# Layer 0's first sample in its own PSUM banks and TensorE's order as written: convolution attention, gated scan attention and expert layer on one core

## The chip, the cores and the metric

One core of a Trainium2 chip runs the whole kernel. The metric is device time in microseconds (us) of that core, lower is better. The median of three runs stands for a kernel; a profiled execution is one further run with the hardware profiler on, and has a time of its own.

## The reference, cut to what matters

The input is `x` of shape (4, 128, 64, 64): four samples, 128 channels, 4096 positions. Layer 0 is an attention over positions whose queries, keys and values come from 1x1 convolutions of the group-normed input:

```python
v = group_norm(x)                                  # 32 groups, over the whole sample
e1 = prelu(w1 @ v + b1)      # (4, 64, 4096)
e2 = prelu(w2 @ v + b2)      # (4, 64, 4096)
asm = prelu(wa @ v + ba)     # (4, 128, 4096)
score = softmax(einsum('nci,ncj->nij', e1, e2), axis=2)
x = x + einsum('nij,ncj->nci', score, asm)
```

Layer 1 takes the positions as tokens `t`: `t = t + attn(norm(t))`, where attn is a running softmax over time with 8 heads (keys and values are `silu` of projections, scores are key times a fixed query per head, outputs are cumulative sums divided by cumulative weights, averaged over heads); then `t = t + ffn(norm(t))`, where 64 experts each pick their 8 best tokens per sample, pool them, and run a two-layer network whose result is added back to the picked tokens. All is in float32.

## The kernel before

**Layer 0.** A sample is cut into 8 query blocks of 512 positions (`BLK`). For each block `qb` there are 16 steps `p`; a step handles 256 key positions as two halves of 128. Three functions make a step: `probs` multiplies keys by queries into a PSUM tile `sc` (two banks), ScalarE exponentiates it to `pr` and VectorE adds `pr` to the running sums `acc`; `weigh` multiplies the values `am` by `pr` into two accumulators `av`. Scores contract over 64 rows, and `weigh` splits its 128 rows in two halves, so both use half of the PE array each and run two at a time. The loop over `steps` issues `probs` of the next step ahead of `weigh` of the present one. After 16 steps `collect` copies `av` out (L604 on ScalarE, L605 on VectorE), and the next block's step 9 calls `finish`.

**Preparation of a sample.** `preparation(b)` returns work for one sample: `stat` (statistics of 512 columns, L442), `chain0` to `chain2` (group means and roots, by two tiny matmuls with `gavg`), and for each block k of 512 columns `normal` (xn, L470), `project` and `value`. `project(k)` multiplies the normed block by both small weights (L495), then biases it on ScalarE (L501, y), takes the PReLU in parts (L478 or L482, L483, L484) to `ee`, and sends it by four copies (L513, L514) to the tiles `e1` (queries of block k) and `e2` (keys of blocks' steps 2k and 2k+1). `value(k)` does eight matmuls of 128 columns (L525), adds the bias on VectorE (L537, ya), and takes the PReLU to `am` (L482 and L483 on ScalarE, L484 on VectorE). The three later samples are prepared inside the loop, one piece at steps 2, 6 and 10 of a query block, from half-array matmuls. The first sample is prepared in the open: the input comes in four transfers of 512 KB (L391) on the queues of SP and ScalarE in turn, two blocks are prepared before the first step, and blocks 2 to 7 inside the first query block, block p/2 + 2 at each even step p, ahead of the step's `weigh`. For this sample `project` and `value` share one PSUM tile `whole` of two banks, out of the pool `ps_x`:

```python
if not whole:
    whole.append(ps_x.tile([P, 2, BLK], F32, tag="x", name=f"whole_{b}"))
pe = whole[0]
nc.tensor.matmul(pe[:, 0, :], w12, xn, start=True, stop=True)
```

`value` takes `whole[0][:, 1:]`. [...]

**What sets the order.** Every engine runs its instructions in a fixed order. A planner chooses that order when the program is built: among instructions whose inputs it takes to be ready, it goes by the order of the source, so work that is ready early moves ahead. `tc.issue_after(i)` puts what it encloses behind instruction i on i's engine. `tc.manual_schedule(engines={PE})` gives TensorE the source's order for what it encloses; before, that held for the last step of layer 0 and for layer 1, and all the rest of layer 0 was left to the planner. Waits for data and for buffers are added by the framework: a tile is handed on when all that reads it has finished.

**Layer 1.** A loop over 32 blocks of 512 tokens, in TensorE's written order. `keys` makes one 128x512 projection per head (L361) into a PSUM tile of the pool `ps_kv`, which has three banks, and ScalarE applies Silu (L362); `scan` takes the running maximum, an Exp on ScalarE (L839), the running sum and a reciprocal; `weights` transposes the scan's result (L880); `values` makes the value projections through the same three banks (L916, L920); `totals` and `outputs` write to the pools `ps_t` and `ps_o`, two banks each. In block 0 the second half of the keys of block 1 (heads 4 to 7) is computed after `scan(0)` has begun and before `weights(0)`. The expert layer comes last.

Of the kernel before, what the change touches and what calls it, by code (L numbers as in the profile page):

```python
# [8 lines left out]
F32 = mybir.dt.float32  # L9
AF = mybir.ActivationFunctionType  # L10
ALU = mybir.AluOpType
AX = mybir.AxisListType
PSUM = bass.MemoryType.PSUM
P = 128
# [4 lines left out]
def conv_attn_hybrid_kernel(  # L19
# [23 lines left out]
    nc = tc.nc  # L43
    B, C, N = x.shape
    R = w1t.shape[1]
    NH = qt.shape[1]
# [4 lines left out]
    BLK = 512  # L51
# [10 lines left out]
    def opener(stack, pre=""):  # L62
        def open_pool(name, bufs=1, **kw):
            return stack.enter_context(
                tc.tile_pool(name=pre + name, bufs=bufs, reuse_waits="tile", **kw)
            )
        return open_pool
# [286 lines left out]
            nc.tensor.transpose(ptr[:, c // 2, :, c % 2, :], xl, ident)  # L354
        return nc.scalar.copy(xt, ptr.rearrange("p q s u j -> p (q s u j)")).ins

    def keys(n, xt, heads, kss, ps, pre=""):

        for h in heads:
            pk = ps.tile([P, BLK], F32, tag="kv", name=f"{pre}pk_{n}_{h}")  # L360
            nc.tensor.matmul(pk, wks[:, h, :], xt, start=True, stop=True)  # L361
            nc.scalar.activation(kss[h], pk, AF.Silu)  # L362
        return [kss[h] for h in heads]
# [8 lines left out]
    with ExitStack() as l0:  # L372
# [7 lines left out]
        wp = pool("l0w")  # L380
        tmp = pool("l0tmp", 2)
        small = pool("l0small", 2)
        ps_x = pool("l0x", space=PSUM)
        ps_av = pool("l0av", space=PSUM)
        qs_p = pool("l0q", NBLK + 1)

        def load_x(b, queues):
            xs = one.tile([P, N], F32, tag="x", name=f"x_{b}")
            for q in range(4):
                cols = bass.ts(q, N // 4)  # L390
                queues[q % len(queues)].dma_start(out=xs[:, cols], in_=x[b, :, cols])  # L391
            return xs

# [28 lines left out]

        gavg = wp.tile([P, P], F32, tag="gavg", name="gavg")
        make_block_diagonal(nc, gavg, C // 32)
        nc.vector.tensor_scalar_mul(gavg, gavg, 32.0 / C)

        queries, keys_of, values_of, sent = {}, {}, {}, []

        def preparation(b):
# [11 lines left out]
            def stat(k):  # L441
                nc.vector.bn_stats(stats[:, k, :], xs[:, bass.ts(k, BLK)])  # L442

            def chain0():
                nc.vector.bn_aggr(mv, stats)

            def chain1():
                pg = ps_x.tile([P, 2, BLK], F32, tag="x", name=f"pg_{b}")
                nc.tensor.matmul(pg[:, 0, 0:1], gavg, mv[:, 0:1], start=True, stop=True)
                nc.vector.tensor_copy(gst[:, 0:1], pg[:, 0, 0:1])  # L450
                nc.vector.tensor_sub(gst[:, 1:2], mv[:, 0:1], gst[:, 0:1])
                nc.vector.scalar_tensor_tensor(
                    out=gst[:, 2:3], in0=gst[:, 1:2], scalar=gst[:, 1:2], in1=mv[:, 1:2],
                    op0=ALU.mult, op1=ALU.add,
                )

            def chain2():
                pg = ps_x.tile([P, 2, BLK], F32, tag="x", name=f"pg2_{b}")
                nc.tensor.matmul(pg[:, 0, 0:1], gavg, gst[:, 2:3], start=True, stop=True)
                i = nc.scalar.activation(std[:, 0:1], pg[:, 0, 0:1], AF.Sqrt, bias=eps5)  # L460
                nc.vector.reciprocal(std[:, 1:2], std[:, 0:1])
                return i.ins

            xn_of = {}

            whole = []

            def normal(k):
                xn = prep.tile([P, BLK], F32, tag="xn", name=f"xn_{b}_{k}")
                nc.vector.tensor_scalar(  # L470
                    out=xn, in0=xs[:, bass.ts(k, BLK)], scalar1=gst[:, 0:1],
                    scalar2=std[:, 1:2], op0=ALU.subtract, op1=ALU.mult,
                )
                xn_of[k] = xn

            def prelu(dst, y, z, minus_a, negative):
                if negative is nc.vector:
                    nc.vector.tensor_scalar(  # L478
                        out=z, in0=y, scalar1=-1.0, scalar2=0.0, op0=ALU.mult, op1=ALU.max
                    )  # L480
                else:
                    nc.scalar.activation(z, y, AF.Relu, scale=-1.0)  # L482
                nc.scalar.activation(y, y, AF.Relu)  # L483
                nc.vector.scalar_tensor_tensor(  # L484
                    out=dst, in0=z, scalar=minus_a, in1=y, op0=ALU.mult, op1=ALU.add
                )

            def project(k):

                xn = xn_of[k]  # L490
                if b == 0:
                    if not whole:
                        whole.append(ps_x.tile([P, 2, BLK], F32, tag="x", name=f"whole_{b}"))
                    pe = whole[0]
                    nc.tensor.matmul(pe[:, 0, :], w12, xn, start=True, stop=True)  # L495
                else:
                    pe = ps_x.tile([P, 2, BLK], F32, tag="x", name=f"pe_{b}_{k}")
                    for u, h in enumerate(halves):
                        nc.tensor.matmul(pe[:, u, :], w12[h, :], xn[h, :], start=True, stop=True)
                y = prep.tile([P, BLK], F32, tag="y", name=f"y_{b}_{k}")  # L500
                nc.scalar.activation(y, pe[:, 0, :], AF.Identity, bias=b12)  # L501
                if b > 0:
                    nc.vector.tensor_add(y, y, pe[:, 1, :])
                z = prep.tile([P, BLK], F32, tag="z", name=f"z_{b}_{k}")
                ee = prep.tile([P, BLK], F32, tag="ee", name=f"ee_{b}_{k}")
                prelu(ee, y, z, neg[:, 0:1], nc.vector if (b, k) == (0, 0) else nc.scalar)
                e1 = qs_p.tile([P, BLK], F32, tag="e1", name=f"e1_{b}_{k}")
                queries[b, k] = e1

                queues = (nc.sync, nc.scalar) if (b, k) == (0, 0) else (nc.sync, nc.sync)  # L510
                by = ee.rearrange("r (j u p) -> r j u p", u=2, p=P)
                for u, (h, queue) in enumerate(zip(halves, queues)):
                    queue.dma_start(out=e1[h, :], in_=ee[halves[0], :])  # L513
                    moved = queue.dma_start(  # L514
                        out=e2[h, bass.ts(k, CPB // 2), :], in_=by[halves[1], :, u, :]
                    )
                if (b, k) != (0, 0):
                    sent.append(moved.ins)

            def value(k):  # L520
                xn = xn_of[k]
                if b == 0:
                    pa = whole[0].rearrange("p u (c d) -> p u c d", c=CPB)[:, 1:]
                    for c in range(CPB):
                        nc.tensor.matmul(  # L525
                            pa[:, 0, c, :], xn[:, bass.ts(c, P)], was, start=True, stop=True
                        )
                else:
                    pa = ps_x.tile([P, 2, CPB, C], F32, tag="x", name=f"pa_{b}_{k}")
                    for c in range(CPB):  # L530
                        for u, h in enumerate(halves):
                            nc.tensor.matmul(
                                pa[:, u, c, :], xn[h, bass.ts(c, P)], was[h, :],
                                start=True, stop=True,
                            )
                y = prep.tile([P, CPB, C], F32, tag="y", name=f"ya_{b}_{k}")
                nc.vector.tensor_tensor(  # L537
                    y, pa[:, 0], bas.unsqueeze(1).to_broadcast([P, CPB, C]), ALU.add
                )
                if b > 0:  # L540
                    nc.vector.tensor_add(y, y, pa[:, 1])
                z = prep.tile([P, CPB, C], F32, tag="z", name=f"za_{b}_{k}")
                prelu(am[:, bass.ts(k, CPB), :], y, z, neg[:, 1:2], nc.scalar)

            first = [lambda k=k: stat(k) for k in range(NBLK)] + [chain0]
            chain = [chain1, chain2]
# [6 lines left out]
        def work_off(blocks, n):  # L553
            for pre, f in blocks[:n]:
                pre()
                f()
            del blocks[:n]
# [100 lines left out]
        with tc.issue_after(root):  # L658
            nc.scalar.activation(seed[:, 1:2], eps5, AF.Exp)
        own = blocks  # L660
        work_off(own, 4)
        nxt = probs(*steps[0])
        first_sums(0, 0, nxt)
# [2 lines left out]
        end = l0.enter_context(ExitStack())  # L666
        for n, (b, qb, p) in enumerate(steps):
            pr = nxt
            if own and p % 2 == 0:
                work_off(own, 2)  # L670
                if not own:
                    with tc.issue_after(sent[-1]):
                        xs_of[1] = load_x(1, (nc.sync,))
            if n + 1 < len(steps):
                nxt = probs(*steps[n + 1])
            if n + 2 == len(steps):
# [3 lines left out]
                for i in range(2):  # L680
                    last_turned = turned(i, xls[i], xts[i], early_room[1])
            weigh(b, qb, p, pr)

            q0 = 1 if b == 0 else 0
            if (qb, p) == (q0, 0) and b + 1 < B:
# [80 lines left out]
    def layer1(pre, ready):  # L766
# [6 lines left out]
        with ExitStack() as kept, ExitStack() as l1:  # L773
# [337 lines left out]
            def loop():  # L1111
# [8 lines left out]
                for n in range(NB):  # L1120
# [7 lines left out]
                    if n + 2 < NB:  # L1128
                        xls = tokens(n + 2, xl_place)
                    if n == 0:  # L1130
                        ks += keys(n + 1, xt_of[n + 1], range(NH // 2, NH), kss, ps_kv, pre)
                    es, rr, _ = made
                    ems = weights(n, es)
                    if n >= 2:
# [391 lines left out]
```

## Time and profile before

| what | us |
|---|---|
| median of three runs (2395.74 to 2397.02) | 2396.14 |
| the profiled execution's own time | 2395.19 |
| its span, first to last instruction | 2393.5 |
| first score matmul (L567) starts | 24.96 |
| copy of the first query block's result (L604) starts | 87.37 |
| end of a query block without preparation to the next one's | 42.53 |
| TensorE idle before the key of head 5 of block 1 (L361) | 2.02 |

The profile's rows give a start and a duration in us, the engine, the source line, what is written from what, and in brackets how long the engine had been idle and what ended that. "PE" rows are matmuls, "PEld" rows are weight loads; every float32 matmul of the source shows as two instructions (x2). SPq and ACTq are the issues of DMAs on those queues. In tables of windows the columns are: window, its length, busy time of PE, PEld, DVE, ACT and POOL with instruction counts, the granted TensorE clock, the DMA share and GB/s.

### The profile page before, as it was taken

The numbers are of one execution on the slowest core, as the hardware profiler recorded it, in microseconds if no ns is written. First come the engines' busy times: TensorE is split into PE (matmuls) and PEld (weight loads), VectorE is DVE, ScalarE is ACT, GpSimd is POOL, SyncE is SP. The second block draws the span as 40 slices with busy tenths as digits, with TensorE's granted clock in tenths as the row PEclk, the third lists the DMA queues.
The fourth block names the chain that finished last, engine by engine and source line by source line (L and its number), as shares of the span: only waits on it lengthen the run. The fifth ranks groups of instructions, "written<-read, shape, count | busy, mean of one in ns | idle before, by whom it ended". The sixth has DMA issues, their size and how long they took to land.

```text
span 2393.5 us, 45621 instructions
## 1 busy us (share of the span) xinstructions
PE 2347.4 (98%) x19416; PEld 1556.4 (65%) x19416; DVE 1493.6 (62%) x2594; ACT 1208.1 (50%) x1639; POOL 301.4 (13%) x337
## 2 busy tenths in 40 slices
PE   7999999999999999999999999999999999999887
PEld 3467767677778677778777775555555555655553
DVE  5666666666655666655555556666666677776655
ACT  5454444444443444444443435666666666666541
POOL 0000000000000000000000001343343433333300
PEclk9999999999999999999999999999999999999999
DMA  3200020001110000020000000212112121112388
GB/s 81 75 23 14 23 62 1 12 18 23 49 25 1 12 18 23 14 56 1 1 1 1 1 1 19 55 38 52 41 38 55 38 51 42 38 38 55 118 309 318
DMA packets 61189, 109.93 MB, mean 46 GB/s; under 512 B 10032, under 2 KB 35120, under 8 KB 60976
## 3 DMA queue, kind: packets, MB, share of 16 engines
q1 hardware_dynamic: 57536, 101.22, 14.7%
q10 hardware_dynamic: 3440, 5.70, 0.7%
q8 instruction: 154, 2.52, 0.4%
q14 instruction: 59, 0.48, 0.1%
HBM read 85.40 MB, written 8.91 MB: 39 GB/s over the span
## 4 chain that ended last, share of the span: by engine, by line


## 5 line engine op out<-in xcount | busy, mean ns | idle before, releaser
L592 PE MATMUL av<-pr,am 64*128 64x512 f32 x4096 | 1066.2, 591 | 0.0
L571 ACT ACTIVATE pr<-sc 128x1024 f32<-128x1024 f32 x512 | 523.2, 1022 | 676.5 <-PE sc L567 607.7
L574 DVE TENSOR_TENSOR acc<-acc,pr 128x1024 f32<-128x1024 f32 x480 | 586.7, 1222 | 440.4 <-ACT pr L571 440.3
L592 PEld LDWEIGHTS av<-pr,am 64*128 64x128 f32 x4096 | 637.8, 187 | 260.3 <-issue 46.8
L567 PE MATMUL sc<-e,e 64*128 64x512 f32 x2048 | 629.3, 593 | 0.0
L567 PEld LDWEIGHTS sc<-e,e 64*128 64x128 f32 x2048 | 320.2, 187 | 107.6 <-issue 24.5
L361 PE MATMUL pk<-room,wks 128*128 128x512 f32 x512 | 241.1, 610 | 2.6 <-ACT room L362 2.4
L916 PE MATMUL pv<-wvs,room 128*128 128x512 f32 x512 | 226.4, 595 | 2.3 <-ACT v L920 2.3
L920 ACT ACTIVATE v<-pv 128x512 f32<-128x512 f32 x256 | 152.5, 597 | 69.9 <-PE pv L916 69.9
L362 ACT ACTIVATE room<-pk 128x512 f32<-128x512 f32 x256 | 148.0, 597 | 56.7 <-PE pk L361 56.4
L916 PEld LDWEIGHTS pv<-wvs,room 128*128 128x128 f32 x512 | 97.0, 191 | 121.0 <-issue 113.3
L806 POOL MEMSET ew<- 128x1024 f32 x1 | 1.0, 951 | 1364.4 <-PE av L592 1364.4
L904 DVE TENSOR_TENSOR em<-em,rb 128x1024 f32<-128x1024 f32 x64 | 78.4, 1225 | 151.0 <-DMA rb<-rd 150.9
L361 PEld LDWEIGHTS pk<-room,wks 128*128 128x128 f32 x512 | 90.5, 190 | 109.4 <-issue 80.3
L895 POOL TENSOR_TENSOR em<-et,mask 128x1024 f32<-128x1024 f32 x64 | 122.6, 1935 | 82.2 <-ACT et L882 82.2
L952 PEld LDWEIGHTS po<-v,em 64*64 64x64 f32 x4096 | 113.1, 134 | 29.5 <-DVE before L942 26.7
L96 POOL TENSOR_SCALAR xg<-t,gmv,grs 128x128 f32<-128x128 f32 x120 | 94.8, 802 | 287.3 <-DVE grs L92 199.3
L952 PE MATMUL po<-v,em 64*64 64x128 f32 x4096 | 121.1, 273 | 2.5 <-issue 2.5
L854 DVE RECIPROCAL rr<-rr 128x512 f32<-128x512 f32 x32 | 107.3, 3353 | 1.1
L839 ACT ACT_TABLE_LOAD x24 | 30.8, 1283 | 119.8 <-DVE ss L838 119.8
L942 DVE TENSOR_TENSOR before<-before,pt 128x128 f32<-128x128 f32 x256 | 72.5, 283 | 9.6 <-PE pt L932 3.8
L849 DVE TENSOR_TENSOR_SCAN rr<-ones,state,ss 128x512 f32<-128x512 f32 x28 | 42.0, 1502 | 48.1 <-ACT ss L839 48.1
(199 smaller groups left out, 2025.7 us busy)
## 6 DMA issues: line engine op xcount, KB each, us to landing
rb<-rd SPq DMA_DIRECT2D x128, 256.0 KB
fw<-in_fw_dram SPq DMA_DIRECT2D x40, 512.0 KB
room<-in_fw_dram SPq DMA_DIRECT2D x18, 512.0 KB
t<-in_xtok_dram SPq DMA_DIRECT2D x32, 256.0 KB
e<-ee SPq DMA_DIRECT2D x63, 128.0 KB
x<-in_x_dram SPq DMA_DIRECT2D x14, 512.0 KB
e<-ee SPq DMA_DIRECT2D x63, 64.0 KB
out_dram<-t SPq DMA_DIRECT2D x8, 256.0 KB
```

The lines of the kernel that those rows point to most:

```text
L96: i = engine.tensor_scalar(out=dst, in0=t[:, chunk, :], scalar1=mean, scalar2=rs, op0=ALU.subtract, op1=ALU.mult)
L361: nc.tensor.matmul(pk, wks[:, h, :], xt, start=True, stop=True)
L362: nc.scalar.activation(kss[h], pk, AF.Silu)
L567: nc.tensor.matmul(sc[:, u, :], e2[halves[u], p, :], e1[halves[u], :], start=True, stop=True)
L571: nc.scalar.activation(pr, sc, AF.Exp)
L574: added.append(nc.vector.tensor_add(acc, acc, pr).ins)
L592: nc.tensor.matmul(av, am[h, j, :], pr[h, u, :], start=(j == 0), stop=(j == NCH - 1))
L854: inverse = nc.vector.reciprocal(rr, rr).ins
L895: nc.gpsimd.tensor_tensor(em, eq.unsqueeze(2).to_broadcast([P, 2 * NH, H2]), mask.unsqueeze(1).to_broadcast([P, 2 * NH, H2]), ALU.mult,)
L916: nc.tensor.matmul(pv.rearrange("p h d -> p (h d)"), xt[:, bass.ts(2 * q + s, P)], wvs[:, bass.ts(m, BLK)], start=True, stop=True,)
L920: last = nc.scalar.activation(v[:, bass.ts(m, HPB), :], pv, AF.Silu).ins
L952: nc.tensor.matmul(po[s * H2 : (s + 1) * H2, u, q, :], aas[q][half, s, h, :], vs[2 * q + s][half, h, :], start=(q == 0 and h == 0), stop=F ...
```

## The change

Five things are altered.

1. For the first sample, `project` and `value` get a tile each (`pe`, `pa`, one bank each) in a pool of their own, `ps_first`, which is closed after block 7; `ps_x` is opened then, in its place. The later samples keep `ps_x`.
2. From the first preparation block to the end of the first query block TensorE takes the order as written, and the preparation of a block comes after the step's `weigh`, not ahead of it: `probs(p+1)`, `weigh(p)`, `project(k)`, `value(k)`.
3. On VectorE, xn of block 2 is put behind `ee` of block 0, xn of block 3 behind `am` of block 0, and ya of block 0 behind `ee` of block 0.
4. The first sample's input comes in eight transfers of 256 KB, and the scaling of `gavg` moves from VectorE to GpSimd.
5. In layer 1's block 0, the keys of heads 4 and 5 of block 1 go to a bank of `ps_o` and one of `ps_t`, which nothing uses yet; heads 6 and 7 go to `ps_kv`.

```diff
-    def keys(n, xt, heads, kss, ps, pre=""):
+    def keys(n, xt, heads, kss, ps, pre="", banks=None):
         for h in heads:
-            pk = ps.tile([P, BLK], F32, tag="kv", name=f"{pre}pk_{n}_{h}")
+            if banks:
+                pk = banks.pop(0)
+            else:
+                pk = ps.tile([P, BLK], F32, tag="kv", name=f"{pre}pk_{n}_{h}")
...
-        ps_x = pool("l0x", space=PSUM)
         ps_av = pool("l0av", space=PSUM)
+        l0first = l0.enter_context(ExitStack())
+        ps_first = opener(l0first)("l0xfirst", space=PSUM)
...
-            for q in range(4):
-                cols = bass.ts(q, N // 4)
+            m = NBLK if b == 0 else 4
+            for q in range(m):
+                cols = bass.ts(q, N // m)
...
-        nc.vector.tensor_scalar_mul(gavg, gavg, 32.0 / C)
+        nc.gpsimd.tensor_scalar_mul(gavg, gavg, 32.0 / C)
...
+            def two_banks(name):
+                if b == 0:
+                    return ps_first.tile([P, 1, BLK], F32, tag="pe", name=name)
+                return ps_x.tile([P, 2, BLK], F32, tag="x", name=name)
...
+            scaled, valued = [], []
             def normal(k):
...
+                    if b == 0 and 2 <= k <= 3:
+                        order.enter_context(tc.issue_after((scaled, valued)[k - 2][0]))
...
             def project(k):
                 xn = xn_of[k]
+                pe = two_banks(f"pe_{b}_{k}")
...
-                    pa = whole[0].rearrange("p u (c d) -> p u c d", c=CPB)[:, 1:]
+                    pa = ps_first.tile([P, 1, CPB, C], F32, tag="pa", name=f"pa_{b}_{k}")
...
+                    if (b, k) == (0, 0):
+                        order.enter_context(tc.issue_after(scaled[0]))
                     nc.vector.tensor_tensor(
                         y, pa[:, 0], bas.unsqueeze(1).to_broadcast([P, CPB, C]), ALU.add
...
+        written = ExitStack()
+        written.enter_context(tc.manual_schedule(engines={mybir.EngineType.PE}))
         work_off(own, 4)
         nxt = probs(*steps[0])
...
             pr = nxt
-            if own and p % 2 == 0:
-                work_off(own, 2)
-                if not own:
-                    with tc.issue_after(sent[-1]):
-                        xs_of[1] = load_x(1, (nc.sync,))
+            if (b, qb, p) == (0, 1, 0):
+                written.close()
...
             weigh(b, qb, p, pr)
+            if own and p % 2 == 0:
+                work_off(own, 2)
+                if not own:
+                    with tc.issue_after(sent[-1]):
+                        xs_of[1] = load_x(1, (nc.sync,))
+                    l0first.close()
+                    ps_x = pool("l0x", space=PSUM)
...
                     if n == 0:
-                        ks += keys(n + 1, xt_of[n + 1], range(NH // 2, NH), kss, ps_kv, pre)
+                        banks = [
+                            ps.tile([P, 2, BLK], F32, tag=tag, name=f"{pre}pk_{tag}")[:, 0, :]
+                            for ps, tag in ((ps_o, "o"), (ps_t, "t"))
+                        ]
+                        ks += keys(
+                            n + 1, xt_of[n + 1], range(NH // 2, NH), kss, ps_kv, pre, banks
+                        )
```

## The prediction

> **What bounds the kernel now.** I read the busy shares first, then the times between the query blocks' copies (L604), then a table of windows, then TensorE's timeline where they differ.
>
> ```profile
> PE 2347.4 (98%) x19416; PEld 1556.4 (65%) x19416; DVE 1493.6 (62%) x2594; ACT 1208.1 (50%) x1639; POOL 301.4 (13%) x337
> ```
> ```profile
> 24.96:87.37 62.41, 62.41 (x257) 28.58 (x258) 35.45 (x42) 36.54 (x50) 0.00 (x0) 1.00 0.39 103
> 1366.87:1409.40 42.53, 42.53 (x218) 31.84 (x216) 23.26 (x33) 16.95 (x17) 0.00 (x0) 1.00 0.00 1
> ...
> 1472.00:1473.00 1.00, 1.00 (x2) 0.43 (x2) 1.00 (x1) 0.21 (x2) 0.00 (x0) 0.50 0.00 0
> 1473.00:1474.00 1.00, 1.00 (x2) 0.23 (x1) 0.18 (x1) 0.46 (x1) 0.00 (x0) 0.50 0.00 0
> ```
>
> TensorE sets the time: a plain query block takes 42.53 us, and a step's 12 half-array instructions take 2.57 (exponentials at 81.30 and 83.87), 0.43 a pair; 16 steps are 41.1. The first query block, with six preparations of 1.71 (two instructions of 512 columns at 0.43, eight of 128 at 0.107), should take 52.3 from its first scores (17 scores at 0.86, 16 weighs at 1.71, 10.3 of preparation) and takes 62.4, though PE shows as busy throughout. The timeline tells where it goes:
>
> ```profile
> 60.68 1.12 PE L495 MATMUL whole<-xn,w 128*128 128x512 f32 x2
> 61.73 1.12 PE L567 MATMUL sc<-e,e 64*128 64x512 f32 x2
> 62.79 1.16 PE L525 MATMUL whole<-was,xn 128*128 128x128 f32 x8
> 63.87 0.69 PE L567 MATMUL sc<-e,e 64*128 64x512 f32 x1
> ```
>
> Between the two full-array pieces stands half a score, two instructions that run alone (1.06 for what costs 0.43 in pairs), because the value waits for y. Each change between half and full array costs 0.2 more. From one projection to the next (60.68 to 69.22) it is 8.54, against 5.14 + 1.71 = 6.85. The start has waits of the same kind, and in layer 1 there is one wait:
>
> ```profile
> 17.21 2.08 PE L525 MATMUL whole<-was,xn 128*128 128x128 f32 x8 [0.78 <-ACT y L501]
> 19.33 0.69 DVE L537 TENSOR_TENSOR ya<-whole,bas 128x512 f32<-128x512 f32 x1 [1.71 <-PE whole L525]
> 19.93 0.74 DVE L484 SCALAR_TENSOR_TENSOR ee<-z,neg,y 128x512 f32<-128x512 f32 x1
> ...
> 24.96 2.08 PE L567 MATMUL sc<-e,e 64*128 64x512 f32 x4
> ...
> 1470.31 4.22 PE L361 MATMUL pk<-room,wks 128*128 128x512 f32 x6 [2.02 <-ACT room L362]
> ```
>
> Here ee sits behind ya on VectorE although its input was there at 18.29, and key head 5 waits for a bank whose Silu stands behind two table loads.
>
> **The input in eight, gavg on GpSimd.** The data arrive up to 8.3, from 3 on at some 400 GB/s (DMA view of the first 30 us); four statistics of 0.62 are still to do then (8.41 to 10.88), with eight pieces two: 1.2 earlier, 0.1 more without gavg ahead of the aggregate. But ScalarE's queue issues two more pieces at 0.45 ahead of its nine weight loads, so its table load moves from 10.29 to 11.19 and the root cannot start before 11.19 + 1.28 + 0.20 = 12.7 (13.25 now): at most 0.55 earlier. The loads of a12 end 0.9 later as well, by 12.1 at the latest (they had landed by 11.20); if the planner leaves L416 ahead of the copy at 11.96, the chain is 0.25 later. Between -0.55 and +0.25 I take -0.3. SP's next item, e's copy, comes ten us later, and GpSimd has idle room for 0.80 (its L96 row); both are free. Here a rule speaks against: the Trainium skill, "DMA: Bandwidth & Descriptors", wants DMAs of 1 MiB or more (Bandwidth) and gives 2.0 us plus bytes over 436 GB/s for each (Anatomy of one DMA, for GpSimd's path). Were these queued one behind the other, four pieces of 256 KB per queue would take 10.4 us where two of 512 KB take 6.4: 4 us later. The trace has four pieces overlapping at 400 GB/s, which leaves one fixed part; I follow it, and keep a possible microsecond of this in the range.
>
> **Blocks 0 and 1.** With ee ahead of ya it starts at 18.3, not 19.93: 1.6, and 1.9 with the chain. Its copies issue at 18.85 (20.70 now) and their data end at 22.0 (23.9 now). TensorE with two banks runs 14.1 project, 16.1 value, 18.2 project, 20.2 value, to 22.2 even at the slow rate of this stretch (2.04 to 2.08 a piece). First scores: 22.3 instead of 24.96. The waits added on VectorE hold nothing up: ya behind ee ends at 19.5, before TensorE comes to the value that needs its bank; xn of blocks 2 and 3, behind ee and am, is done by 23 and wanted at 27 and 35. They should cost 1.1 and not 2.08: before, TensorE ran without a gap from 22.95 and was fast at 28.41; now it runs without one from 14.1. The exponential ends at 24.6, and weigh(0) starts at 24.7.
>
> **Blocks 2 to 7.** From there to the block's end TensorE has 16 weighs at 1.71 (27.4), 15 scores at 0.86 (12.9), six preparations at 1.71 (10.3), and six changes of array shape at 0.87 (0.64 into the full array, with a last unpaired instruction, and 0.23 out, both from 60.68 to 69.22): 55.8, so L604 at 80.5 instead of 87.37, 6.9 earlier. A projection comes each 7.7 us, not 8.54. Does anything arrive late? From the start of project(k): y 1.16 to 1.85, z and the second Relu to 3.17, ee to 3.95 where VectorE is free; in the block at 60.68 the copies' data ended 3.6 after ee (65.38 to 69.0), so at 7.6. They are needed by probs(2k), after 7.7 + 1.9 = 9.6. Now the distance is about 14 (L495 of block 3 at 35.05, scores of step 6 near 49), and other matmuls could move ahead; in written order nothing can. xn is no issue: it is made a block ahead (39.68 for 43.59 and later). ScalarE has five activations (3.2 us) and two exponentials (2.0) in 7.7; in the order y, z, Relu, za, ya the exponential of step 2k-2 ends at 5.5 where its weigh wants it at 5.5: I charge 0.15 a block, 0.9. Sum of the first block: 6.0.
>
> The moves around it are free: x of sample 1, issued at 76.44 behind the last copy, moves up with it (four issues on SP as now); the pool in ps_x's place is first used at step 11 of the next query block, 30 us after block 7's readers; GpSimd's mask and qz work shifts by 0.8 and is wanted at 78 and later. Plain blocks stay at 42.5, there is nothing in them to gain or lose.
>
> **Keys.** Heads 4 and 5 no longer wait. Head 6 takes head 1's or 4's old bank, free at 1466.4; head 7 waits for head 2's Silu, 1469.66 + 0.60. TensorE reaches it at 1469.7 and idles 0.6, not 2.02. The Silus then follow each other from 1469.66 (three in 1.57) and the first value matmul starts when head 6's is done, 1472.4, instead of 1475.11: 2.7. Most of it rests on the granted clock, 0.50 from about 1471.6 to 1475.0: the wait of 2.02 cost 1.7 more by slow matmuls. The Trainium skill, "TensorE: Matmul & The Clock Gate", Part 1, closes the gate after an idle window of about 3.4 us; by it so short a wait costs itself alone, and the edit would bring 1.4. The trace shows the slow clock after 2.02, and full speed through waits of 0.6 (1493 to 1495), so I take 2.7. Behind it, em's product (1483.33) waits for rb, whose data end at 1482; its second half, at 1484.87 now, can come 2.7 earlier but no more.
>
> **Sum.** 6.0 + 2.7 = 8.7 off the profiled 2395.19 gives 2386.5; the median of the runs lies 0.95 above that execution, so 2387.5.
>
> **Rivals.** *A late key block turns the gain into a loss.* On VectorE the planner may put ee behind ya and behind a running sum (1.22) whose exponential stands behind za and ya: ee then ends at 8.0, the copies land at 11.6, and TensorE idles 2.0 in every one of six blocks, which also closes the clock gate as at 1471 (1.7 more): 22 us, 2395.2 - 8.7 + 22 + 1 = 2409. It decides from an end of ee at 8.0 after project's start; up to 6.0 it costs nothing. Now ee ends 4.7 after, against it; for it, the written order has no way round. *The same, mildly:* ee ends at 6.5 to 6.9, 0.6 to 1.0 us a block, 4 to 6 in all: 2391.5 to 2393.5. Now the xn and acc rows do lie between its parts. *Keys or banks do nothing:* if the wait isn't for the bank but the gate closes after 0.6 too, keys bring 1; or value waits for y though it has a tile of its own, and blocks stay near 8.1: about 2390 in both cases. The row names y and the shared tile, against it.
>
> **How the numbers follow.** Forecast 0.70 (2384 to 2390.5), mild lateness 0.15, keys or banks without effect 0.10, heavy lateness 0.05. A measurement here tells 0.2%, 4.8 us, from no change: faster is below 2391.3. Forecast and the third case count as faster, the mild one mostly as same: 0.81, 0.13, 0.06. Range 2383.5 to 2393: below, cheap changes of shape (0.31 for 1446.59 to 1447.76 instead of 0.64, 2 in all) and the full 0.55 of the chain; above, most of the mild case.
>
> **What would show it.** Right: L604 first at 80 to 82, first L567 near 22.3, L495 to L495 7.6 to 7.9 with L525 directly behind it, no idle of TensorE before L567, L361's longest wait at 0.6 and the clock at 1.00 around 1472. Wrong: idle before scores ended by a DMA of e, ee later than 6 us behind L495, root later than 13.5, or plain blocks off 42.5.

## The result and the profile after

The changed kernel takes 2385.19 us, median of six runs (2383.88 to 2387.11); the kernel before took 2396.53 in the six runs beside them. The ratio is 0.9954, with a 95% interval from 0.9941 to 0.9967: about 11 us less (7.9 to 14.1 by the interval), where 8.7 were forecast. The profiled execution took 2384.92 us, its span is 2383.2. Lines are numbered anew: L507 is project, L538 value, L583 the scores, L608 weigh, L620 the block's copy, L364 the keys, L365 their Silu, L938 the value projections of layer 1. (A row's x8 at value is four matmuls of the source, two instructions each.)

First the busy line of the page, then the table of windows, with the first query block, a plain block, and slices of 1 us (columns as before; the clock is the third number from the right):

```profile
PE 2340.1 (98%) x19416; PEld 1554.0 (65%) x19416; DVE 1494.8 (63%) x2593; ACT 1208.1 (51%) x1639; POOL 304.2 (13%) x338
```
```profile
22.25:79.19 56.94, 56.94 (x256) 27.85 (x258) 36.62 (x43) 36.76 (x50) 0.00 (x0) 0.97 0.38 101
1358.68:1401.21 42.53, 42.53 (x218) 31.80 (x216) 23.28 (x33) 16.97 (x18) 0.00 (x0) 1.00 0.00 1
...
23.00:24.00 1.00, 1.00 (x4) 0.46 (x2) 1.00 (x2) 0.00 (x0) 0.00 (x0) 0.50 0.00 0
...
1463.00:1464.00 1.00, 0.68 (x5) 0.36 (x3) 1.00 (x1) 1.00 (x4) 0.00 (x0) 1.00 0.00 0
```

The busy share of TensorE is 98% as before and tells nothing. The first block takes 56.94 instead of 62.41 and starts 2.71 earlier; its end moves from 87.37 to 79.19, by 8.18. Plain blocks take 42.53 to the hundredth, so that the end of layer 0 moves by the same amount (1453.26 to 1445.07). Then comes the place of the keys, where the clock now stays at 1.00. But at 23 the clock column reads 0.50, where it read 1.00 before. That does not mean full speed before: the four score instructions at 24.96 took 2.08 there, against 1.13 for the four at 36.79 below, and the eight value instructions at 17.21 took 2.08, against 1.05. At the start of these profiles the column reads 1.00 while the durations show the slow rate; there the durations are what to read. The timeline of a middle preparation, and of the start:

```profile
34.84 1.12 PE L507 MATMUL pe<-xn,w 128*128 128x512 f32 x2
35.81 1.05 PE L538 MATMUL pa<-was,xn 128*128 128x128 f32 x8
36.79 1.13 PE L583 MATMUL sc<-e,e 64*128 64x512 f32 x4
...
42.14 1.12 PE L507 MATMUL pe<-xn,w 128*128 128x512 f32 x2
```
```profile
17.79 0.75 DVE L498 SCALAR_TENSOR_TENSOR ee<-z,neg,y 128x512 f32<-128x512 f32 x1 [0.70 <-ACT y L497]
18.46 0.69 DVE L553 TENSOR_TENSOR ya<-pa,bas 128x512 f32<-128x512 f32 x1
...
19.20 1.16 PE L538 MATMUL pa<-was,xn 128*128 128x128 f32 x8
...
22.25 3.65 PE L583 MATMUL sc<-e,e 64*128 64x512 f32 x8 [1.90 <-DMA e<-ee]
...
25.68 1.94 PE L608 MATMUL av<-pr,am 64*128 64x512 f32 x8
```

Project and value stand back to back, the lone half score between them is gone, and from one project to the next it is 7.30 instead of 8.54. At the start `ee` is ahead of `ya`, and the first scores begin at 22.25 instead of 24.96. But TensorE now has nothing to do for 1.90 ahead of them, and the eight instructions then take 3.65.

In layer 1 the keys of heads 6 and 7 and the first value projections:

```profile
1462.12 1.13 PE L364 MATMUL pk<-room,wks 128*128 128x512 f32 x2 [0.31 <-ACT room L365]
...
1464.07 6.28 PE L938 MATMUL pv<-wvs,room 128*128 128x512 f32 x14 [0.40 <-ACT room L365]
```

The wait of 2.02 has become 0.31, and 0.40 ahead of the values. From the running maximum's matmuls (start at 1461.88 before, 1453.68 now) to the values it took 13.23 and takes 10.39: 2.84 less, which with the 8.18 puts the values 11.04 earlier. This lead does not last. The outputs' matmuls start at 1486.33 before and 1475.39 now, 10.94 earlier, and in the next block TensorE waits 1.39 for a key's bank where it did not wait before. First before, then now:

```profile
1491.01 3.74 PE L361 MATMUL pk<-room,wks 128*128 128x512 f32 x8
...
1498.45 1.88 PE L916 MATMUL pv<-wvs,room 128*128 128x512 f32 x4
```
```profile
1484.45 1.12 PE L364 MATMUL pk<-room,wks 128*128 128x512 f32 x2 [1.39 <-ACT room L365]
...
1489.29 7.03 PE L938 MATMUL pv<-wvs,room 128*128 128x512 f32 x16
```

The next block's value projections are only 9.16 earlier: of the 2.84, 1.88 are given back, and 0.96 stay. The Silu waited for stands on ScalarE behind the next block's Exp, and that behind its running maximum on VectorE, whose last step starts at 1488.95 before and 1479.78 now, 9.17 earlier. The planner's order on VectorE ahead of it is another one: em's first product stood ahead of a reciprocal (L92: em at 1483.33, the reciprocal at 1484.46) and now stands behind it (1473.51, after 1.04 of idle time for ScalarE, and em at 1473.78). That this order is the cause has not been tested. The experts' first matmul is 10.8 earlier; the 1.6 more arise in code that the change does not touch.

### The profile page after: what moved, and what is told of

It reads as the page before. It is cut to its first block, busy times and chain, and to the rows that moved or that the text cites. A ratio compares the mean times of both kernels' runs of the same rounds, so it can differ in the third digit from the quotient of the medians.

```text
span 2383.2 us, 45629 instructions
## 1 busy us (share of the span) xinstructions
PE 2340.1 (98%) x19416; PEld 1554.0 (65%) x19416; DVE 1494.8 (63%) x2593; ACT 1208.1 (51%) x1639; POOL 304.2 (13%) x338
## 4 chain that ended last, share of the span: by engine, by line
## 5 line engine op out<-in xcount | busy, mean ns | idle before, releaser
L608 PE MATMUL av<-pr,am 64*128 64x512 f32 x4096 | 1057.2, 591 | 0.0
L608 PEld LDWEIGHTS av<-pr,am 64*128 64x128 f32 x4096 | 634.6, 187 | 260.4 <-issue 45.2
L583 PE MATMUL sc<-e,e 64*128 64x512 f32 x2048 | 618.9, 594 | 1.9 <-DMA e<-ee 1.9
L583 PEld LDWEIGHTS sc<-e,e 64*128 64x128 f32 x2048 | 317.3, 188 | 106.5 <-issue 19.5
L364 PE MATMUL pk<-room,wks 128*128 128x512 f32 x508 | 238.3, 607 | 2.0 <-ACT room L365 1.7
L938 PE MATMUL pv<-wvs,room 128*128 128x512 f32 x512 | 227.0, 596 | 2.5 <-ACT v L942 2.1
L938 PEld LDWEIGHTS pv<-wvs,room 128*128 128x128 f32 x512 | 97.0, 191 | 121.9 <-issue 114.2
L365 ACT ACTIVATE room<-pk 128x512 f32<-128x512 f32 x254 | 146.8, 597 | 54.4 <-PE pk L364 54.2
L364 PEld LDWEIGHTS pk<-room,wks 128*128 128x128 f32 x508 | 89.4, 189 | 107.6 <-issue 79.0
```

The lines of the kernel that those rows point to most:

```text
L583: nc.tensor.matmul(sc[:, u, :], e2[halves[u], p, :], e1[halves[u], :], start=True, stop=True)
L608: nc.tensor.matmul(av, am[h, j, :], pr[h, u, :], start=(j == 0), stop=(j == NCH - 1))
L938: nc.tensor.matmul(pv.rearrange("p h d -> p (h d)"), xt[:, bass.ts(2 * q + s, P)], wvs[:, bass.ts(m, BLK)], start=True, stop=True,)
```

## The experiments

This table has a profile's milestones for each kernel, in us: the square root that ends the chain of statistics, the first scores, the first block's end, the time from the running maximum to the first value projection ("keys"), from there to the first value projection of layer 1's next block ("next"), and from the first value projection to the experts' first matmul ("rest", which holds "next"). The rest has the same source in all kernels.

| kernel | median (n) | ratio to before [95%] | root | first scores | block end | keys | next | rest |
|---|---|---|---|---|---|---|---|---|
| before | 2396.53 (6) | | 13.25 | 24.96 | 87.37 | 13.23 | 23.34 | 825.6 |
| before_again | 2396.61 (1) | | 13.1 | 24.8 | 86.5 | 13.25 | 23.34 | 826.7 |
| keys_alone | 2395.16 (12) | 0.9993 [0.9984, 1.0002] | 13.2 | 24.9 | 87.5 | 10.39 | 25.21 | 830.1 |
| order_alone | 2398.12 (20) | 1.0008 [1.0001, 1.0014] | 13.0 | 24.7 | 88.34 | 11.55 | 23.33 | 826.8 |
| banks_alone | 2386.53 (4) | 0.9957 [0.9941, 0.9974] | 13.45 | 23.85 | 78.34 | 11.55 | 23.49 | 829.7 |
| after | 2385.19 (6) | 0.9954 [0.9941, 0.9967] | 12.72 | 22.25 | 79.19 | 10.39 | 25.22 | 825.8 |
| after_again | 2386.66 (1) | | 12.56 | 22.11 | 78.02 | 10.39 | 25.21 | 829.4 |
| late_block | 2411.54 (4) | 1.0065 [1.0048, 1.0082] | 12.8 | 22.35 | 103.3 | 10.39 | 25.20 | 826.1 |
| planner_order | 2385.57 (5) | 0.9957 [0.9944, 0.9971] | 12.7 | 22.23 | 77.7 | 10.39 | 25.22 | 829.7 |
| fill_gap | 2387.20 (5) | 0.9963 [0.9950, 0.9976] | 12.5 | 24.36 | 78.7 | 10.40 | 25.21 | 828.1 |
| four_pieces | 2384.76 (4) | 0.9953 [0.9938, 0.9969] | 13.26 | 22.64 | 79.7 | 10.40 | 25.21 | 826.3 |
| keep_warm | 2382.77 (5) | 0.9943 [0.9930, 0.9957] | 12.88 | 23.17 | 79.42 | 10.39 | 25.21 | 824.6 |
| planner_four | 2387.60 (5) | 0.9964 [0.9950, 0.9977] | 12.66 | 22.18 | 77.67 | 15.01 | 24.37 | 826.9 |
| warm_one | 2381.50 (5) | 0.9943 [0.9929, 0.9956] | 12.60 | 22.13 | 78.06 | 10.40 | 25.21 | 822.8 |

The last column is the warning for all that follows: the rest differs by up to 7.3 us between profiles, and by 3.6 between two of the same program. One part of this, "next", is systematic: it is 23.3 to 23.5 in the four profiles without part 5, and 25.2 in all with it, but planner_four (24.37). The kernel before stood at 2395.8 to 2396.5 beside each of them. The totals tell 10 us from nothing; for a single part of the change the milestones are the better measure.

### Which part brings it: keys, order, banks, each alone

keys_alone is the kernel before with part 5 only (cut here; the two banks are handed in as in the change):

```diff
-            pk = ps.tile([P, BLK], F32, tag="kv", name=f"{pre}pk_{n}_{h}")
+            if banks:
+                pk = banks.pop(0)
+            else:
+                pk = ps.tile([P, BLK], F32, tag="kv", name=f"{pre}pk_{n}_{h}")
...
```

> The kernel before with the fifth part alone: keys of heads 4 and 5 of block 1 in banks of ps_o and ps_t. If a wait of 2.02 us also costs the slow clock that follows it: first value matmul (L916) 2.7 to 2.9 us earlier against score(0), granted clock 1.00 from 1470 to 1476, total 2.3 to 2.9 us less (some of it lost again where em waits for rb). If a wait costs only itself: 1.4 us less and the clock still at 0.50 for some microseconds. First query block unchanged, L604 at 87.4.

The total, expected 2.3 to 2.9 us less, moved by about 1 us, with an interval that holds no change. The keys took 10.39, as in the changed kernel, so the 2.84 are there at their place. But the next block gives 1.87 of them back by the same wait of 1.39 as above, and 0.97 stay, which fits the total. The rest of its profile is 4.5 longer than that of before, with these 1.87 in it.

order_alone is the kernel before with the written order and the preparation behind `weigh`, on the shared tile:

```diff
+        written = ExitStack()
+        written.enter_context(tc.manual_schedule(engines={mybir.EngineType.PE}))
         work_off(own, 4)
...
             weigh(b, qb, p, pr)
+            if own and p % 2 == 0:
+                work_off(own, 2)
```

> The kernel before with TensorE's written order in the first query block and preparation behind weigh, on the one shared tile; no other part. If the banks carry the gain: in written order TensorE waits for y between project and value (1.1 to 1.3 us idle a block) where the planner had half a score to put there, so L495 to L495 is 8.3 to 8.6 and the first block is as before or slower, 0 to 3 us. If the order carries it: 7.5 or less and L604 near 82.

It is slower, by 1.9 us in the median (0.2 to 3.4). Its timeline shows what the planner's half score had been good for: in the written order nothing moves into the wait for y, and project to project is 8.34.

```profile
38.80 1.13 PE L495 MATMUL whole<-xn,w 128*128 128x512 f32 x2
40.70 1.16 PE L525 MATMUL whole<-was,xn 128*128 128x128 f32 x8 [0.78 <-ACT y L501]
```

banks_alone is the kernel before with part 1 only, TensorE's order left to the planner:

```diff
-                    pe = whole[0]
+                    pe = ps_first.tile([P, 1, BLK], F32, tag="pe", name=f"pe_{b}_{k}")
...
-                    pa = whole[0].rearrange("p u (c d) -> p u c d", c=CPB)[:, 1:]
+                    pa = ps_first.tile([P, 1, CPB, C], F32, tag="pa", name=f"pa_{b}_{k}")
```

> The kernel before with the pool of two tiles pe and pa for the first sample alone; TensorE's order left to the planner, preparation still ahead of weigh, no other part. If the banks carry the gain of the first block: L495 to L495 7.3 to 7.5 us as in the changed kernel, L604 of the first block at 79.5 to 81, total 6 to 8 us less. If the written order carries it: the distance stays above 8 us, L604 at 85 or later.

It brings 9.7 us of the 11, more than the 6 to 8 expected, and the first block ends at 78.34, 9.0 earlier. With nothing to wait for, the planner itself puts value directly behind project:

```profile
31.45 1.13 PE L498 MATMUL pe<-xn,w 128*128 128x512 f32 x2
32.41 1.05 PE L528 MATMUL pa<-was,xn 128*128 128x128 f32 x8
33.39 1.13 PE L570 MATMUL sc<-e,e 64*128 64x512 f32 x4
```

So the written order is not what makes the period short. To see what it does in the changed kernel, planner_order takes it out there and puts the preparation ahead of `weigh` again:

```diff
-        written = ExitStack()
-        written.enter_context(tc.manual_schedule(engines={mybir.EngineType.PE}))
...
             pr = nxt
+            if own and p % 2 == 0:
+                work_off(own, 2)
```

> The changed kernel without its second part: TensorE's order left to the planner and preparation ahead of weigh as before, all else kept. If the written order is worth nothing or costs: block 2's project and value fill the gap in which the scores wait for the copies of e, the clock stays at 1.00 from 20 to 27, first L604 at 77 to 78.3 (79.19), total 1 to 2 us below the changed kernel. If the written order carries part of the gain: L604 at 80 or later.

The block ends at 77.7, 1.5 earlier than after, and the total is the same (2385.57). The 1.5 arise at the start: the planner puts the projection of block 2 ahead of the first scores, TensorE waits 0.74 there and not 1.90, and its clock stays at 1.00.

### The input in eight

four_pieces is the changed kernel with four transfers and the scaling of `gavg` on VectorE:

```diff
-            m = NBLK if b == 0 else 4
+            m = 4
...
-        nc.gpsimd.tensor_scalar_mul(gavg, gavg, 32.0 / C)
+        nc.vector.tensor_scalar_mul(gavg, gavg, 32.0 / C)
```

> The changed kernel without its fourth part: input in four transfers and gavg on VectorE. If the eight transfers are worth what the chain shows: root (L471) at 13.2 to 13.3 instead of 12.72, all of the first block 0.5 later, L604 at 79.7, total 0.5 more. If the input's arrival does not matter because ScalarE's table load sets the root: L604 within 0.2 of 79.19.

Root 13.26 instead of 12.72, first scores 0.39 and block end 0.5 later. Part 4 is worth half a microsecond; the total can't show it, and the pieces and gavg's move were not taken apart. The smaller pieces lost nothing. That is against the rule of 1 MiB or more in the Trainium skill's page "DMA: Bandwidth & Descriptors" (Bandwidth), which the prediction weighed; the page measured it on GpSimd's path, and these transfers go by the queues of SP and ScalarE.

### The heavy rival, built

late_block prepares the next block one step later, at odd p, so that the copies of `ee` have less time until their scores:

```diff
-            if own and p % 2 == 0:
+            if own and p % 2 == 1:
                 work_off(own, 2)
```

> The changed kernel with the preparation of a block one step later (at odd steps). The scores of step 2k then stand 4.6 us behind the start of project(k) in TensorE's order, where the copies of e land about 7.5 behind it (ee ends at 4.0, 3.5 for the copies). By the forecast's rival of a late block: TensorE idles 2.9 to 3.3 us before L583 in each of six blocks, ended by a DMA of e, and the granted clock falls to 0.50 after each, 1.7 more: 26 to 30 us over the changed kernel. If the idle does not touch the clock: 18 to 20 us over it.

It takes 2411.5 us, 26 more than after and 15 more than before. The waits (per line: total us, times, longest) and two of them in the timeline:

```profile
PE sc L583 <- DMA e<-ee: 14.8, 11, 2.8
```
```profile
37.65 1.09 PE L583 MATMUL sc<-e,e 64*128 64x512 f32 x2 [1.88 <-DMA e<-ee]
...
39.80 3.67 PE L608 MATMUL av<-pr,am 64*128 64x512 f32 x7
...
50.08 1.09 PE L583 MATMUL sc<-e,e 64*128 64x512 f32 x2 [1.90 <-DMA e<-ee]
...
51.90 2.30 PE L608 MATMUL av<-pr,am 64*128 64x512 f32 x7
```

So a wait of this kind is one loop step away. The two stretches differ in what follows the same wait: after 1.88 the seven weigh instructions take 3.67, after 1.90 they take 2.30. Of the seven idle times of 1.88 to 2.76 in this block, the one before the first scores among them, three were followed by the slow clock (from 22, 39 and 63 on). The total lies in the expected 26 to 30 over after, but its terms do not: the long waits are 1.88 to 2.76, not 2.9 to 3.3, and the clock fell after two of these six, not after each. The waits are 12.9 us more than in after, the two slow stretches under 4, and the first block 24.1 longer; what is left goes, as far as the rows show, with instructions that run alone, as at 50.08. That the sum came out is luck.

### The idle time before the first scores

fill_gap prepares three blocks, not two, before the first step:

```diff
-        work_off(own, 4)
+        work_off(own, 6)
```

> The changed kernel with three blocks prepared ahead of the first step instead of two, written order kept. If the idle of 1.90 us before the first scores and the slow clock after it (22.4 to 25.5) are what the written order costs: no idle over 1 us there, clock 1.00, first L604 0.5 to 1.5 us earlier than 79.19. If the values' bank of block 2 comes late (its ya reads at 23.4): the gap only moves, and L604 is within 0.4 of 79.19.

The idle time was not filled but cut into waits of 1.33, 1.0 and 0.67, and the scores began 2.1 later. The clock stayed up and the block ended at 78.7. The total (2387.2) shows no gain.

keep_warm puts two matmuls behind value(1), whose result nothing reads:

```diff
         work_off(own, 4)
+        idle = ps_first.tile([P, 1, BLK], F32, tag="pe", name="idle")
+        for _ in range(2):
+            nc.tensor.matmul(idle[:, 0, :], w12, xs_of[0][:, :BLK], start=True, stop=True)
```

> The changed kernel with two more 128x512 matmuls (four instructions, some 1.9 us) issued behind value(1), into the idle bank pe; their result is not read. Theory (the idle of 1.90 us at 20.36 lets the granted clock fall to 0.50 at 22.4 to 25.5): the idle before the first scores shrinks below 0.5 us, the clock stays at 1.00, the eight score instructions take 1.9 us instead of 3.65, and the first query block ends 1.0 to 1.5 us earlier, at 77.7 to 78.2 instead of 79.19. Rival (the slow clock at this place comes from something else than the idle, as it came in only some of the longer idles): the clock falls at 22 all the same and the block ends at 79.2 to 79.5. Total by the theory 2384, by the rival 2385.4.

Half a miss: the clock stayed at 1.00 and the scores took 1.99, but the block ended at 79.42. The bank was the wrong one: its reader y was not done, the first of the two waited 0.74 for it, and the scores came at 23.17. warm_one takes one matmul and a bank that nobody uses yet:

```diff
         work_off(own, 4)
+        idle = ps_av.tile([P, BLK], F32, tag="av1", name="idle")
+        nc.tensor.matmul(idle, w12, xs_of[0][:, :BLK], start=True, stop=True)
```

> The changed kernel with one more 128x512 matmul (two instructions, 0.86 us at full speed) behind value(1), this time into a bank of the accumulators that nothing uses yet, so that it waits for nothing; its result is not read. Theory (the idle before the first scores alone takes the clock away): the matmul runs at 20.4 to 21.3, the idle of 1.90 shrinks to about 0.9, the granted clock stays at 1.00 from 20 to 28, the first scores still start near 22.2, and the first query block ends at 77.7 to 78.2, 1.0 to 1.5 earlier than 79.19. Rival (the drop doesn't hang on this idle): the clock falls all the same and the block ends near 79.2. The total may hide it, since the same program twice ended its experts' start 2.4 us apart: 2382 to 2386.

```profile
20.45 1.02 PE L681 MATMUL idle<-x,w 128*128 128x512 f32 x2
22.13 2.08 PE L583 MATMUL sc<-e,e 64*128 64x512 f32 x8 [0.65 <-DMA e<-ee]
24.46 1.99 PE L608 MATMUL av<-pr,am 64*128 64x512 f32 x8 [0.26 <-ACT pr L587]
```

Now the scores take 2.08, weigh(0) starts at 24.46, and the block ends at 78.06, 1.13 earlier than after. With 2381.5 us (2379.88 to 2383.40) it has the lowest median of all. Its ratio and that of after overlap, though, and its profile has the rest at 822.8, 3.0 below that of after, which one matmul at 20 us doesn't explain. Nor are the 1.13 shown to be the matmul's, as the next run tells.

after_again is the changed kernel unchanged, one run:

> The changed kernel once more, unchanged. If an idle of 1.9 us at 20.4 closes the clock gate each time, the granted clock falls to 0.50 at 22.4 to 25.5 again and the first block ends at 79.2; if it is open which of such short idles closes it, the clock may stay at 1.00 and the block end at 77.7 to 78. Time 2385.

```profile
22.11 2.08 PE L583 MATMUL sc<-e,e 64*128 64x512 f32 x8 [1.66 <-DMA e<-ee]
24.44 1.99 PE L608 MATMUL av<-pr,am 64*128 64x512 f32 x8 [0.26 <-ACT pr L587]
```

The same program, an idle time of 1.66 instead of 1.90, no slow clock, and the block ends at 78.02. This corrects the readings above. Against 78.02, planner_order gains 0.3 and not 1.5, fill_gap loses 0.7, keep_warm loses 1.4, and warm_one gains nothing (78.06): the clock stayed up here without its matmul. banks_alone is only 0.3 behind: beside separate tiles, parts 2 to 4 together move the first block's end by some tenths. At the first value projection of layer 1's next block banks_alone (1487.12) is even ahead of after_again (1488.13) and after (1489.29).

before_again is the kernel before, unchanged, to see whether its wait of 2.02 is always followed by the slow clock:

> The kernel before, profiled once more. The wait of 2.02 us before key head 5 was followed by a granted clock of 0.50 in the profile of before, and by none in two kernels that kept that wait. If the slow clock belongs to the length of the wait, it is there again and the first value matmul (L916) stands 13.2 us behind score(0). If it depends on where the wait falls against something that the program does not set, it may be absent, and L916 stands 11.4 to 11.6 behind score(0).

It did: 0.50 from 1470 to 1473, and 13.25 for the keys. In order_alone and banks_alone the same wait of 2.02 stands, and the six key instructions behind it took 2.84 at clock 1.00, for 11.55 in all:

```profile
1460.52 2.84 PE L361 MATMUL pk<-room,wks 128*128 128x512 f32 x6 [2.02 <-ACT room L362]
```

So of the 2.84 that part 5 brings at its place, 1.16 (11.55 to 10.39) come from the wait, and 1.7 only where the clock would have fallen. With the next block in, keys and "next" together take 36.57 in before, 35.04 in banks_alone and 35.61 in after: part 5 is worth 1.0 against the profiles where the clock fell, and loses 0.6 against banks_alone, where it did not.

### Four keys in the unused banks

planner_four is planner_order with all four keys in the two tiles of two banks each:

```diff
-                            ps.tile([P, 2, BLK], F32, tag=tag, name=f"{pre}pk_{tag}")[:, 0, :]
-                            for ps, tag in ((ps_o, "o"), (ps_t, "t"))
+                            two[:, u, :] for two in [
+                                ps.tile([P, 2, BLK], F32, tag=tag, name=f"{pre}pk_{tag}")
+                                for ps, tag in ((ps_o, "o"), (ps_t, "t"))
+                            ] for u in range(2)
```

> The changed kernel with TensorE's order in the first block left to the planner (preparation issued ahead of weigh, as in planner_order), and with all four keys of heads 4 to 7 of block 1 in the four unused banks of ps_o and ps_t. Theory: heads 6 and 7 wait for no bank (0.31 now), the values wait only for the Silus of heads 1 to 3; from the first running-maximum matmul to the first value matmul it takes 9.4 to 10.0 us instead of 10.39; 0.3 of it is lost again where em's product waits for rb. The total would be 2385, at most 0.7 below planner_order (2385.57), which the totals hardly tell. Rival (the values wait for ScalarE's Silus behind two table loads, whatever the banks are): 10.39 stays.

Both theories missed. The keys take 15.01, 4.6 more:

```profile
1456.81 1.02 PE L364 MATMUL pk_o<-room,wks 128*128 128x512 f32 x2
1460.83 1.75 PE L364 MATMUL pk_o<-room,wks 128*128 128x512 f32 x2 [3.00 <-ACT room L365]
```

The second head writes the other bank of the same tile and waits 3.00 for the Silu that reads the first bank. It is the wait of the kernel before (value for y, in the other bank of `whole`) built a second time: in both places what is waited for is the tile, and not the bank.

### Why the rest differs in the same program

These rows are from the last scan block of after and of after_again, TensorE's timeline of each:

```profile
2240.78 5.29 PE L938 MATMUL pv<-wvs,room 128*128 128x512 f32 x8
2248.17 3.70 PE L938 MATMUL pv<-wvs,room 128*128 128x512 f32 x8 [2.10 <-ACT v L942]
...
2258.85 3.27 PE L974 MATMUL po<-v,em 64*64 64x128 f32 x108 [1.86 <-issue]
```
```profile
2240.35 3.93 PE L938 MATMUL pv<-wvs,room 128*128 128x512 f32 x8
2247.75 5.40 PE L938 MATMUL pv<-wvs,room 128*128 128x512 f32 x8 [3.47 <-ACT v L942]
...
2260.82 4.94 PE L974 MATMUL po<-v,em 64*64 64x128 f32 x108 [2.56 <-issue]
```

In after the clock was low at 2240 to 2245. The matmuls took 1.36 longer there, and the wait for ScalarE behind them was 1.37 shorter: free. Then the clock stayed up. In after_again the matmuls ran at full speed into a wait of 3.47, after which eight took 5.40; after 2.56 the outputs took 4.94. From 0.43 ahead it fell to 3.64 behind (the next transposes start at 2263.96 and 2267.60). keys_alone, banks_alone and planner_order have the same pattern as after_again, with waits of 3.46 to 3.47 and 5.40 behind them, and rests of 829.7 to 830.1. In keys_alone this makes the stretch of these values 2.1 longer than in before (12.63 for 10.56); of the 4.5 by which its rest is longer, that and the 1.87 of the next block are the two main terms.

## Why the prediction came out

The sign was right, and so was the main mechanism: waits that come from shared tiles and banks. The sum, 8.7, is 2.6 below the measured 11.3 and within its interval. It came out in part by luck, as terms that were too small stand against one that was too large. In the profile the 10.8 at the experts' first matmul are 8.2 of the first block, 1.0 of the keys, and 1.6 that arise behind them in code that no part touches (in after_again's profile that stretch is 1.9 longer than in before).

Of the signs that it named, the first scores (22.25) and the clock at 1472 came. The first block's end (79.19 for 80 to 82) and the period (7.30 for 7.6 to 7.9) were better than they should be, and TensorE's idle time ahead of the first scores, ended by a DMA of e, was a sign of being wrong that did come, once. By its steps:

- **Chain of statistics.** Root at 12.72, 12.95 forecast. ScalarE's table load starts at 11.06, the small activation behind it ends at 12.56, as the bound had it (12.7); the root follows after 0.16 more, for the matmul of the means.
- **First scores.** 22.25 for 22.3. The step that failed is "now it runs without one from 14.1": TensorE was already fast at 19.20 (value(1) in 1.16, not 2.04), so it was done at 20.36 and idle for 1.90. The prediction had carried the slow rate on to 22.2. In this execution that cost the clock, and weigh(0) began at 25.68, not 24.7. Where the clock stayed (after_again) it began at 24.44.
- **Period 7.7.** It is 7.30. The mis-sized term is the change of array shape, 0.87 a block. It is 0.45: the starts stand 0.10 to 0.12 further apart at each of four joints (weigh to project, project to value, value to scores, scores to weigh). The 0.64 "into the full array" was read off a place where a split score left an unpaired instruction, and that went with the split. Six blocks: 2.5.
- **Late exponentials.** The 0.9 charged was not seen: from weigh(0) on, TensorE shows no idle time in the block. `ee` ends 3.97 behind project, as said (3.95); the copies' data end near 42.4 for scores at 44.09.
- **First block in sum.** 8.18 for 6.0: 2.5 by shapes and 0.9 by the charge, less 1.0 by the clock at 22, which leaves 0.2 unassigned.
- **Keys.** 2.84 for 2.7 at the place, with waits of 0.31 and 0.40 for the 0.6. The step that failed is the one behind it, put at no loss: "its second half, at 1484.87 now, can come 2.7 earlier". Beside the 8.18 of the block it came 0.67 earlier (1476.02), and the next block's keys then waited 1.39. Of the 2.7 credited, 1.0 reached the next block's values. Also, "full speed through waits of 0.6 (1493 to 1495)" is a misreading: TensorE is busy throughout these two microseconds, and the 0.61 ahead of the Silu at 1496.08 is ScalarE's idle time. That the clock falls after 2.02 held for before and before_again, but it is no rule: by the page "TensorE: Matmul & The Clock Gate" (Part 1) of the Trainium skill, which wants an idle window of about 3.4 us, the gain would have been 1.4, and 1.16 is what remains where the clock stayed up.
- **Credit.** One part of five carries nearly all of it, the separate tiles. The prediction gave the written order a role in the 7.7; banks_alone has 7.29 without it, and order_alone, where tiles are shared, is 1.9 us slower with it.
- **Heavy rival.** It did not occur, as `ee` kept its 3.97. late_block builds a wait like it in another way, with the scores earlier and not `ee` later; its 2411.5 is near the 2409 forecast for the rival, but by other terms, and does not test it.

Open: which short idle time brings the slow clock; why 20 runs of order_alone are 1.9 us slower in the median while the first value projection stands 1.2 earlier in its profile than in before; and what sets VectorE's order behind part 5, and whether it makes the 1.39.

## What to carry to other kernels

Where a matmul waits for a reader of another bank, give it a tile of its own before writing the order by hand: the planner finds the order once the wait is gone, and a written order keeps the wait. Size a cost from a stretch that the change leaves in place, not from one whose odd instruction the change removes. For effects below some 4 us, compare the times of fixed milestones in two profiles, and profile the same program twice, before believing a total or explaining a difference of 1 us. Follow a gain from its place to the same milestone of the next block: here two thirds of it were gone there.

## What the runs showed of the hardware that was not expected

The granted clock fell to 0.50 after idle times of TensorE of 1.75 (four_pieces), 1.88 (late_block), 1.90 (after) and 2.02 (before, twice), and did not fall after 1.66 (after_again), 1.73 (banks_alone), 1.90 and 1.95 (late_block), 2.02 (banks_alone, order_alone) and 2.54 (warm_one, at 2247). Near 2 us it is open in each execution. The price was 1.1 us at the first scores of after and 1.7 at the keys of before, and nothing at 2240 in after, where a wait for ScalarE hid it. That a matmul in the middle of such a gap keeps the clock up is not shown: it stayed up in warm_one, and in after_again without the matmul. At the start of a profile the clock column is no guide: in before it reads 1.00 from 14 to 27 while eight value instructions take 2.08 (17.21), against 1.16 at 62.79.
